# Products of zeros on TensorE in units 14 to 16 of a chunk of a scan-and-attention kernel

## The chip, the cores and the metric

The kernel runs on one core of one Trainium2 chip. The metric is the time on the device in microseconds (us). The engines are named as in the profile: PE is TensorE (PEld its weight loads), DVE is VectorE, ACT is ScalarE, POOL is GpSimd, and SP issues most of the DMAs.

## The reference

The input `x` has eight images of 96 channels and 64 x 64 places, so L = 4096 tokens each. What is computed, in short:

```python
# layer 0: group norm, then a selective scan (16 states, 192 inner channels)
xz = u @ in_proj_w.T                      # split in xm and z
xm = silu(causal_conv4(xm) + conv_b)
dt, Bm, Cm = split(xm @ x_proj_w.T)       # 6, 16 and 16 columns
delta = softplus(dt @ dt_proj_w.T + dt_proj_b)
h[t] = exp(delta[t] * A) * h[t-1] + delta[t] * Bm[t] * xm[t]   # 192 x 16 states
y[t] = sum_n h[t] * Cm[t] + xm[t] * D
x = x + layer_norm((y * silu(z)) @ out_proj_w.T)
# layer 1, on tokens
t = t + linear_attention(layer_norm(t))   # 6 heads, no softmax, so q (k^T v)
t = t + ffn(layer_norm(t))                # 96 -> 384 -> 96, fp8 e5m2 products, fp16 sums
```

## The kernel before, in words

Two images make a pair, and a pair is cut in eight **chunks** of T = 512 tokens: 4 pairs x 8 chunks = 32 chunks. A chunk is worked in 24 **units**. Unit `u` stands for a group `j` of 64 inner channels (3), a group `g` of four states (4), and an image `b` of the pair (2), in this order: `j = u // 8`, `g = (u // 2) % 4`, `b = u % 2`. A unit has two halves `h`, each of 128 rows (4 states x 32 channels) x 512 tokens.

What one unit does (function `unit`, in this order on its engines):

- PE copies the rows of C of the next unit into a PSUM bank (`rows_c`, L715, two banks `cc`), unless the unit is in `POOLED`.
- `steps(u, 0)`: the steps that the table `STEPS` lists before the bar for this unit.
- POOL multiplies delta * x by B three units ahead (`products_b`, L703, `dbu`).
- DVE scans both halves (L800, `hs`). After each half ACT writes the decay of the next unit's half, `exp(delta * A)`, into one of two PSUM banks `da` (`decay`, L725).
- In units 1, 9 and 17: `gate` (L766). DVE multiplies the finished sums of the group before by `silu(z)`.
- `steps(u, 1)`: the steps after the bar. In units 1, 9 and 17 then `skip` (L759): PE opens the bank `y` with `D * x` of the group `j` that begins.
- DVE multiplies the states by C (L823, `pr`), or POOL does so at the beginning of the next unit (`pooled`, L830), where the unit is in `POOLED`.

The **sums** over states are products on PE (`sums`, L747): for two units, four products with a 128 x 32 selection matrix, each added to 32 rows of the bank `y`, which stays open from `skip` until the fourth group of states has been added. A step `S` in the table runs the oldest of them, if its products are there. The bank `y` is single, its last sums are those of units 6 and 7, 14 and 15, 22 and 23, and `s["summed"]` is set to `j` when they have been issued. For j = 1 this happens in the two `S` steps of unit 16, part 0.

The steps of `STEPS` other than `S` advance generators of other work by one stage. The ones near the change:

- `P` (`chain_p`) prepares the chunk after the next: convolution (L491), z (L499), silu, then in units 13 to 17 the product with `x_proj` (L532), its copies on ACT (L537, L540), and three times a product of 12 rows for delta (L550) that ACT reads (L554) before the next can take the one bank `mp`. A softplus with its table loads (L555) follows on ACT.
- `E` (`chain_e`) takes the chunk before through output projection, layer norms and transposes. Its products with the input's tokens (L867) fall in units 13 and 14.
- `F0` and `F1` (`chain_f`) run the attention's output and the FFN of an earlier chunk, from the tenth chunk on. In `F0` the three products of the hidden layer (L1049) come first, then in unit 15 the second product (L1089, three fp8 products into bank `mF`), in unit 16 ACT's copy of it (L1094, `y16`), four transposes on PE (L1101) and the last addition on DVE (L1104).

Each engine works strictly in the order in which the program issues to it; the order is written out by hand in `STEPS` and `unit` (a manual schedule), with semaphores between the engines.

The parts of the table for the units of the change:

```python
    14: "F0 | E E P",
    15: "F0 F0 | P F0",
    16: "S S | P E F0 W1* F1 F0*",
```

Of the kernel before, what the change touches and what calls it, by code (L numbers as in the profile page):

```python
# [10 lines left out]
F16 = mybir.dt.float16  # L11
# [9 lines left out]
T = 512  # L21
# [38 lines left out]
    22: "F1 P F1 |",  # L60
    23: "E | P",
}


PAIRS = sorted({((u // 2) % NG, u % 2) for u in POOLED})
# [7 lines left out]
def tile_mamba_linear_attention_ffn(  # L73
# [29 lines left out]
    nc = tc.nc  # L103
    B, _, L = x.shape
# [4 lines left out]
    const = ctx.enter_context(tc.tile_pool(name="const", bufs=1))  # L109
# [299 lines left out]
    def now(kind):  # L409
        for work in waiting[kind]:  # L410
            work()
        waiting[kind].clear()
# [51 lines left out]
    here = {}  # L464
# [200 lines left out]
    def spread(s, j):  # L665

        if ("inputs", j) in s:
            settle(s["inputs", j])
        for to, of in (("du", "lu"), ("dl", "ld")):
            t = s[to, j] = p2.tile([128, 4, T], F32, tag=to, name=to)  # L670
            for n in range(NG):
                nc.sync.dma_start(
                    t[32 * n : 32 * n + 32],
                    s[of, j].rearrange("(q e) t -> e q t", e=32),
                )

    def rows_b(s, g):

        t = s["b", g] = p2.tile([128, 2, T], F32, tag="b", name="b", bufs=NG)
        for n in range(NG):  # L680
            nc.sync.dma_start(
                t[32 * n : 32 * n + 32],
                s["bd"][0 : 2 * NS].rearrange("(b n) t -> n b t", b=2)[NG * g + n]
                .unsqueeze(0)
                .to_broadcast([32, 2, T]),
            )

    def rows_pooled(s, g, b):

        t = s["c", g, b] = p2.tile([128, T], F32, tag=f"c{g}{b}", name="c", bufs=1)  # L690
        for n in range(NG):
            row = 2 * NS + NS * b + NG * g + n
            nc.sync.dma_start(
                t[32 * n : 32 * n + 32], s["bd"][row : row + 1].to_broadcast([32, T])
            )
# [4 lines left out]
    def products_b(s, u):  # L700
        j, g, b = where(u)
        dbu = s["dbu", u] = p2.tile([128, 2, T], F32, tag="dbu", name="dbu", bufs=AHEAD + 1)
        nc.gpsimd.tensor_mul(  # L703
            dbu, s["du", j][:, 2 * b : 2 * b + 2, :],
            s["b", g][:, b, :].unsqueeze(1).to_broadcast([128, 2, T]),
        )

    def rows_c(s, u):
        j, g, b = where(u)
        if u in POOLED:  # L710
            return
        if ("low", 0) in s:
            settle(s["low", 0])
        cc = s["cc", u] = ps_all.tile([128, T], F32, tag="cc", name="cc", bufs=2)
        nc.tensor.matmul(  # L715
            cc, lhsT=sel[64:128, g, b], rhs=s["cs"][64:128, :], start=True, stop=True
        )

    def decay(s, u, h, bank=None):
        if s is None or ("da", u, h) in s:  # L720
            return
        j, g, b = where(u)
        da = psum(bank) if bank else ps_all.tile([128, T], F32, tag="da", name="da", bufs=2)
        s["da", u, h] = da
        nc.scalar.activation(  # L725
            da, s["dl", j][:, 2 * b + h, :], AF.Exp, scale=aneg[:, 2 * j + h, g : g + 1]
        )
# [26 lines left out]
    def skip(s, j):  # L754

        s["open"] = j

        s["y"] = ps_all.tile([128, T], F32, tag="y", name="y", bufs=1)
        nc.tensor.matmul(  # L759
            s["y"], lhsT=dd[:, j, :], rhs=s["xm"][:, j, :], start=True, stop=False  # L760
        )

    def gate(s, j):
        assert s["summed"] == j
        zs = s["zs"][:, j, :]
        vector().tensor_mul(zs, s["y"], zs)  # L766

    def unit(s, prev, nxt, first, u, steps):
        def at(v):
            return (s, v) if v < NU else (nxt, v - NU)  # L770


        here.update(at=at, u=u, part=0)
        if u - 1 in POOLED:
            pooled(s, u - 1)
        elif not u and NU - 1 in POOLED and prev is not None:
            pooled(prev, NU - 1)
        if u:
            nc.scalar.copy(state["new"][:, u - 1, :], s.pop(("hs", u - 1))[:, :, T - 1])  # L779
        else:  # L780
            if prev is not None:
                nc.scalar.copy(state["new"][:, NU - 1, :], prev.pop(("hs", NU - 1))[:, :, T - 1])
            state["last"] = state.get("new")
            state["new"] = p2.tile([128, NU, 2], F32, tag="state", name="state")
        to, v = at(u + 1)
        if to is not None:
            rows_c(to, v)
        now("norms")
        steps(u, 0)
        to, v = at(u + AHEAD)  # L790
        if to is not None:
            products_b(to, v)
        now("shifts")
        if u % 2:
            due.append((s, u))
        hs = s["hs", u] = p2.tile([128, 2, T], F32, tag="hs", name="hs", bufs=3)
        dbu = s.pop(("dbu", u))
        to, v = at(u + 1)
        for h in range(2):
            nc.vector.tensor_tensor_scan(  # L800
                hs[:, h, :], s.pop(("da", u, h)), dbu[:, h, :],
                0.0 if first else state["last"][:, u, h : h + 1], ALU.mult, ALU.add,
            )
            if to is not None:
                decay(to, v, h)
        between[0] = 0
        now("others")

        new = u % (2 * NG) == 1
        if new and u > 1:  # L810
            gate(s, u // (2 * NG) - 1)
        elif new and prev is not None:
            gate(prev, NJ - 1)
        here["part"] = 1
        steps(u, 1)
        if new:
            skip(s, u // (2 * NG))
        if u in POOLED:
            return
        pr = s["pr", u] = p2.tile([128, 2, T], F32, tag="pr", name="pr", bufs=PRB)  # L820
        cc = s.pop(("cc", u)).unsqueeze(1)
        for lo, hi in ((0, 2),) if between[0] else ((0, 1), (1, 2)):
            nc.vector.tensor_mul(  # L823
                pr[:, lo:hi], hs[:, lo:hi], cc.to_broadcast([128, hi - lo, T])
            )

    def pooled(s, u):
        j, g, b = where(u)
        pr = s["pr", u] = p2.tile([128, 2, T], F32, tag="pr", name="pr", bufs=PRB)
        nc.gpsimd.tensor_mul(  # L830
            pr, s["hs", u], s["c", g, b].unsqueeze(1).to_broadcast([128, 2, T])
        )
# [338 lines left out]
    with tc.manual_schedule():  # L1171
        for u in range(AHEAD):
            products_b(slots[0], u)
        for h in range(2):
            decay(slots[0], 0, h)
        rows_c(slots[0], 0)
        for i, (p, c) in enumerate(chunks):
            s = slots[i]
            prev = slots[i - 1] if i else None
            nxt = slots[i + 1] if i + 1 < N else None  # L1180

            def steps(u, part):
                if part == 0:
                    if u in (0, 2 * NG):
                        spread(s, 1 + u // (2 * NG))
                    if nxt is not None and u == 18:
                        spread(nxt, 0)
                    if nxt is not None and u in ROWS_B:
                        rows_b(nxt, ROWS_B.index(u))
                    for k, v in ROWS_POOLED.items():  # L1190
                        if v % NU == u:
                            to = s if v >= NU else nxt
                            if to is not None and ("c", *k) not in to:
                                rows_pooled(to, *k)
                for name in (STEPS[u] + "|").split("|")[part].split():
                    step(name, i)

            for u in range(NU):
                unit(s, prev, nxt, c == 0, u, steps)
# [4 lines left out]
    s = slots[N - 1]  # L1204
# [285 lines left out]
```

## Time and profile before

| | |
|---|---|
| time, median of 3 runs | 3046.27 us (3036.72 to 3049.2) |
| profiled execution | 3054.44 us |
| its span, first to last instruction | 3052.7 us |
| mean granted TensorE clock | 0.807 |
| instructions in the span | 36480 |
| busiest engines | DVE 2822.1 us, POOL 2784.1 us |

A chunk takes some 90 us of the span, a unit some 3.7 us on the mean. The share of busy time is an average over the whole; what an engine's work is worth in one stretch is read from the waits there. Matmuls are pipelined and their ends are modelled, so that a busy PE row does not say that the array is full. The granted clock is the share of full speed that the core's throttle grants to TensorE, as the profile records it. In rows of the timeline the columns are the start, the duration, the engine, line and operation, what is written and read, the shape, the count of instructions merged, and in brackets the idle time before them with what ended it.

### The profile page before, as it was taken

To read this page: it belongs to the slowest core of one execution; us is meant where nothing else is said; L and a number is where in the kernel's file an instruction comes from. 1 tells how busy PE (TensorE), PEld (TensorE's weight loads), DVE (VectorE), ACT (ScalarE), POOL (GpSimd) and SP (SyncE) were. 2 spreads that over 40 slices of the span, in tenths; PEclk is the share of its full clock that TensorE was granted. 3 is DMA by queue.
4 is the path that set the end of the run, shared out by engine and by line. 5 is a ranking of instruction groups with operands and counts; after the bars stand their busy time and mean duration, and the time that the engine had idled before them with its cause. 6 is when DMAs were issued, how large, how long until landed. Compare 5 with 4: busy or idle time off the path is not lost. (4 is left out here: it accounts for less than half of the span.)

```text
span 3052.7 us, 36480 instructions
## 1 busy us (share of the span) xinstructions
PE 2413.1 (79%) x9663; PEld 931.8 (31%) x9663; DVE 2822.1 (92%) x4499; ACT 2384.0 (78%) x4809; POOL 2784.1 (91%) x1483
## 2 busy tenths in 40 slices
PE   5777777777788887787888778888887888888787
PEld 2122222222233332232333223232233333233355
DVE  4999999999999999999999999999999999999987
ACT  3666666777668888888888887888888888888766
POOL 2999999999999999999999999999999999999947
PEclk9787777777778888879887887888788888878679
DMA  5655666555576755657765556765556675555632
GB/s 138 144 139 139 160 164 160 143 130 128 134 170 173 179 150 147 148 127 170 182 168 142 140 150 152 178 171 143 135 139 145 171 180 144 139 133 129 165 99 78
DMA packets 261238, 452.24 MB, mean 148 GB/s; under 512 B 41701, under 2 KB 50086, under 8 KB 261030
## 3 DMA queue, kind: packets, MB, share of 16 engines
q1 hardware_dynamic: 256038, 447.81, 58.8%
q10 hardware_dynamic: 4992, 2.11, 0.3%
q8 instruction: 76, 1.25, 0.2%
q14 instruction: 132, 1.08, 0.1%
HBM read 357.50 MB, written 92.27 MB: 147 GB/s over the span
## 5 line engine op out<-in xcount | busy, mean ns | idle before, releaser
L703 POOL TENSOR_TENSOR dbu<-du,b 128x1024 f32<-128x1024 f32 x768 | 1828.5, 2410 | 52.0 <-DMA du<-lu 35.9
L800 DVE TENSOR_TENSOR_SCAN hs<-da,state,dbu 128x512 f32<-128x512 f32 x1290 | 1569.7, 1264 | 93.7 <-ACT da L725 92.8
L725 ACT ACTIVATE da<-dl,aneg 128x512 f32<-128x512 f32 x1474 | 989.8, 685 | 480.1 <-DVE hs L800 477.0
L830 POOL TENSOR_TENSOR pr<-hs,c 128x1024 f32<-128x1024 f32 x288 | 686.2, 2383 | 69.7 <-DVE hs L800 43.5
L823 DVE TENSOR_TENSOR pr<-hs,cc 128x512 f32<-128x512 f32 (+1 forms) x766 | 593.5, 805 | 0.0
L747 PE MATMUL y<-pr,ssum 128*32 128x512 f32 x3072 | 541.5, 799 | 4.9 <-POOL pr L830 4.9
L491 PE MATMUL mp<-u,wk 96*64 96x512 f32 x1488 | 420.6, 661 | 69.7 <-ACT xm L509 41.6
L715 PE MATMUL cc<-cs,sel 64*128 64x512 f32 x480 | 270.8, 579 | 3.9 <-DVE pr L823 3.4
L532 PE MATMUL mp<-xm,xpT 128*96 128x512 f32 x186 | 153.6, 993 | 120.1 <-ACT xm L525 77.0
L800 DVE TENSOR_TENSOR_SCAN hs<-da,dbu 128x512 f32<-128x512 f32 x184 | 212.6, 1203 | 25.3 <-ACT da L725 16.0
L550 PE MATMUL mp<-dbl,dtT 12*128 12x512 f32 x186 | 159.0, 948 | 72.4 <-ACT delta L554 36.4
L851 PE MATMUL mE<-woT,zs 128*128 128x192 f32 x744 | 151.0, 357 | 72.3 <-ACT t1e L859 46.9
L491 PEld LDWEIGHTS mp<-u,wk 96*64 96x64 f32 x1488 | 107.9, 146 | 290.2 <-issue 155.0
L759 PE MATMUL y<-xm,dd 128*128 128x512 f32 x192 | 130.1, 765 | 73.5 <-DVE zs L766 73.5
L715 PEld LDWEIGHTS cc<-cs,sel 64*128 64x128 f32 x480 | 100.1, 216 | 275.5 <-issue 168.8
L499 PE MATMUL mp<-u,wz 96*64 96x512 f32 x372 | 115.6, 704 | 63.2 <-ACT zs L522 58.6
L851 PEld LDWEIGHTS mE<-woT,zs 128*128 128x128 f32 x744 | 131.7, 206 | 95.7 <-ACT t1e L859 60.5
L747 PEld LDWEIGHTS y<-pr,ssum 128*32 128x32 f32 x3072 | 88.8, 128 | 211.2 <-issue 183.2
L779 ACT COPY state<-hs 128x2 f32<-128x2 f32 x736 | 133.7, 182 | 1.4
L532 PEld LDWEIGHTS mp<-xm,xpT 128*96 128x96 f32 x186 | 46.4, 270 | 234.1 <-ACT xm L525 129.6
L566 POOL TENSOR_TENSOR du<-delta,xm 128x512 f32<-128x512 f32 x93 | 117.5, 1280 | 0.0
L919 PE MATMUL mE<-t1e 128*97 128x97 f32 x496 | 74.1, 285 | 46.6 <-DVE gram L928 36.4
(326 smaller groups left out, 3272.0 us busy)
## 6 DMA issues: line engine op xcount, KB each, us to landing
du<-lu SPq DMA_DIRECT2D x380, 256.0 KB, 5.0
dl<-ld SPq DMA_DIRECT2D x380, 256.0 KB, 7.4
b<-bd SPq DMA_DIRECT2D x512, 128.0 KB, 3.5
lu<-du SPq DMA_DIRECT2D x96, 256.0 KB, 4.0
c<-bd SPq DMA_DIRECT2D x384, 64.0 KB, 3.5
ld<-delta SPq DMA_DIRECT2D x93, 256.0 KB, 3.0
xg<-in_x_dram SPq DMA_DIRECT2D x32, 384.0 KB, 3.6
xr<-in_x_dram SPq DMA_DIRECT2D x32, 384.0 KB, 8.4
```

The lines of the kernel that those rows point to most:

```text
L491: nc.tensor.matmul(ps[64 * b : 64 * b + 64, :], lhsT=wk[:, k, 64 * j : 64 * j + 64], rhs=u[:, b, k : k + T], start=(k == 0), stop=(k == 3),)
L532: nc.tensor.matmul(ps[0:C, :], lhsT=xpT[:, j, :], rhs=xm[:, j, :], start=(j == 0), stop=(j == NJ - 1),)
L550: nc.tensor.matmul(ps, lhsT=dtT[:, j, :], rhs=dbl[0 : 2 * RANK, :], start=True, stop=True)
L703: nc.gpsimd.tensor_mul(dbu, s["du", j][:, 2 * b : 2 * b + 2, :], s["b", g][:, b, :].unsqueeze(1).to_broadcast([128, 2, T]),)
L715: nc.tensor.matmul(cc, lhsT=sel[64:128, g, b], rhs=s["cs"][64:128, :], start=True, stop=True)
L725: nc.scalar.activation(da, s["dl", j][:, 2 * b + h, :], AF.Exp, scale=aneg[:, 2 * j + h, g : g + 1])
L747: nc.tensor.matmul(s["y"][q : q + 32, :], lhsT=ssum, rhs=pr[:, h, :], start=False, stop=(g == NG - 1),)
L779: nc.scalar.copy(state["new"][:, u - 1, :], s.pop(("hs", u - 1))[:, :, T - 1])
L800: nc.vector.tensor_tensor_scan(hs[:, h, :], s.pop(("da", u, h)), dbu[:, h, :], 0.0 if first else state["last"][:, u, h : h + 1], ALU.mult, ...
L823: nc.vector.tensor_mul(pr[:, lo:hi], hs[:, lo:hi], cc.to_broadcast([128, hi - lo, T]))
L830: nc.gpsimd.tensor_mul(pr, s["hs", u], s["c", g, b].unsqueeze(1).to_broadcast([128, 2, T]))
L851: nc.tensor.matmul(ps[:, 2 * k * C : 2 * (k + 1) * C], lhsT=zs[:, j, tok : tok + 128], rhs=woT[:, j].rearrange("p b c -> p (b c)"), start= ...
```

## The change

Two constants are filled with zeros in the set-up: `zw`, a weight of 128 x 128, and `zx`, an operand of 128 x 512, both in fp16. `zeros(n)` issues `n` products of them onto the open bank `y`, adding nothing to its values. It is called at the start of part 0 (after `rows_c` of the next unit, ahead of the steps) and of part 1 (ahead of the steps) of units 14, 15 and 16, with the counts 1 and 1, 2 and 2, 1 and 1. It returns without a product where no bank is open or the open group's sums have all been issued.

```diff
+ZEROS = {14: (1, 1), 15: (2, 2), 16: (1, 1)}
...
     def skip(s, j):
 
         s["open"] = j
-
+        here["sums"] = s
         s["y"] = ps_all.tile([128, T], F32, tag="y", name="y", bufs=1)
         nc.tensor.matmul(
             s["y"], lhsT=dd[:, j, :], rhs=s["xm"][:, j, :], start=True, stop=False
         )
+
+    zw = const.tile([128, 128], F16, name="zw")
+    nc.vector.memset(zw, 0.0)
+    zx = const.tile([128, T], F16, name="zx")
+    nc.vector.memset(zx, 0.0)
+
+    def zeros(n):
+        s = here.get("sums")
+        if s is None or s.get("summed") == s.get("open"):
+            return
+        for _ in range(n):
+            nc.tensor.matmul(s["y"], lhsT=zw, rhs=zx, start=False, stop=False)
...
         now("norms")
+        zeros(ZEROS.get(u, (0, 0))[0])
         steps(u, 0)
...
         here["part"] = 1
+        zeros(ZEROS.get(u, (0, 0))[1])
         steps(u, 1)
```

## The prediction

> **What bounds the kernel now.** I read the page first, then the chain of waits, then the stretch of units 13 to 19 of some chunks in order of time, and last the granted clock in that stretch. The page's first part and its clock row:
>
> ```profile
> PE 2413.1 (79%) x9663; PEld 931.8 (31%) x9663; DVE 2822.1 (92%) x4499; ACT 2384.0 (78%) x4809; POOL 2784.1 (91%) x1483
> PEclk9787777777778888879887887888788888878679
> ```
>
> VectorE (DVE) is busy for 2822 of 3053 us. TensorE (PE) has room on average, at a mean clock of 0.807. So a change on PE can move the end only where DVE waits. Who waits for whom, in total:
>
> ```profile
> ACT da L725 <- DVE hs L800: 477.0, 707, 4.6
> DVE hs L800 <- ACT da L725: 108.8, 120, 3.0
> DVE zs L766 <- PE y L747: 37.5, 28, 3.6
> ACT y L1094 <- PE mF L1089: 19.0, 39, 2.8
> ```
>
> DVE's scans wait 109 us for ScalarE's decays, its gate 37.5 us for the sums on PE, and ScalarE (ACT) waits 19 us for the FFN's second product. Where these waits stand in a chunk, from the timeline between 2178 and 2196 us:
>
> ```profile
> 2178.38 2.07 PE L550 MATMUL mp<-dbl,dtT 12*128 12x512 f32 x2 [1.09 <-ACT delta L554]
> 2180.39 1.52 PE L1089 MATMUL mF<-h,w2T 128*96 128x512 fp8e5 x3
> 2181.83 2.07 PE L550 MATMUL mp<-dbl,dtT 12*128 12x512 f32 x2
> 2181.94 0.58 ACT L1094 CAST y<-mF 96x512 f16<-96x512 f32 x1 [0.44 <-PE mF L1089]
> 2185.57 3.64 PE L747 MATMUL y<-pr,ssum 128*32 128x512 f32 x16
> 2189.33 0.69 DVE L766 TENSOR_TENSOR zs<-y,zs 128x512 f32<-128x512 f32 x1 [0.97 <-PE y L747]
> 2195.66 2.46 DVE L800 TENSOR_TENSOR_SCAN hs<-da,state,dbu 128x512 f32<-128x512 f32 x2 [0.65 <-ACT da L725]
> ```
>
> The bracket is the idle time before the group. From the first row to the sums (16 records, 3.64 us) PE does one thing after the other. ACT's cast of the FFN result (L1094) waits 0.44 us for PE. From that cast to the scan of unit 19 pass 13.7 us in 20 of the 21 chunks that have this cast and the next chunk's products, and in those 20 ACT has no other gap over 0.06 us on the way. DVE waits 0.97 us at the gate (unit 17) and 0.65 at the scan of unit 19: 1.62 us. In the chunk between 2449 and 2468 us the split is another and the sum the same:
>
> ```profile
> 2454.37 0.58 ACT L1094 CAST y<-mF 96x512 f16<-96x512 f32 x1 [0.44 <-PE mF L1089]
> 2461.05 0.69 DVE L766 TENSOR_TENSOR zs<-y,zs 128x512 f32<-128x512 f32 x1 [0.26 <-PE y L747]
> 2468.10 1.28 DVE L800 TENSOR_TENSOR_SCAN hs<-da,state,dbu 128x512 f32<-128x512 f32 x1 [1.36 <-ACT da L725]
> ```
>
> 0.26 + 1.36 = 1.62. So ACT's unbroken row of work, which starts at L1094, sets when unit 19 is scanned; a gate that opens sooner only makes the scan wait longer. What counts is whether L1094 comes sooner or later.
>
> The clock, in four stretches of 3.41 us (the step in which it changes in this trace) of the chunk from 1904 us; columns are busy time and count of PE, PEld, DVE, ACT, POOL, then the clock and DMA:
>
> ```profile
> 1903.70:1907.11 3.41, 3.31 (x11) 2.53 (x11) 3.11 (x4) 3.38 (x7) 3.25 (x3) 0.50 0.17 56
> 1907.11:1910.53 3.42, 3.42 (x6) 0.93 (x5) 3.42 (x5) 2.95 (x6) 3.42 (x3) 0.50 0.33 99
> 1910.53:1913.94 3.41, 3.41 (x11) 1.13 (x13) 3.41 (x19) 3.36 (x7) 3.41 (x2) 0.50 0.01 2
> 1913.94:1917.35 3.41, 3.41 (x17) 0.47 (x9) 2.56 (x3) 3.38 (x3) 2.92 (x2) 0.50 0.20 58
> ```
>
> PE is busy throughout, and the clock is 0.50 throughout.
>
> **The change, part by part.** *What runs.* Seven products a chunk, not eight: in part 1 of unit 16 the two S steps have just summed group j = 1, so `summed` equals `open` and `zeros` returns. 32 x 7 = 224 products with a weight load each. On PE they stand: two ahead of the second set of token products (L867) in unit 14, two ahead of the FFN's second product (L1089) in unit 15, two ahead of the third delta product (L550), one ahead of the sums in unit 16. The other engines keep their order but for set-up, and no wait is added. Two fills on DVE in the set-up: by the fill of 32x128 at 165 ns and the one of 1024 columns at 912 ns I estimate 0.4 us in all, where DVE waits 17.2 us for its first product anyway: nothing.
>
> *One zero's price.* No f16 product of 512 columns stands in the trace. The nearest is L1089, one byte a value and one record a product: three take 1.52 us, one alone 0.61 to 0.66, so each further one costs (1.52 - 0.62) / 2 = 0.45 us at clock 0.50. The other end is an f32 product, two records 0.85 us apart (L550: 2.07 us for two, 1.22 alone): 1.7 us. The lower end is nothing, in idle time. I take 0.45, since a zero is one record in the program, as L1089 is; 0.22 at clock 1.00.
>
> *Unit 14's pair, 0.9 us.* Idle time ahead of the second L550 follows it: 1.09 us in the chunk shown, 0.87 or more in 16 of the 21 chunks, 0.65 and 0.71 in two, at most 0.1 in three. So it is free in 18 and costs 0.9 us in three. In the first ten chunks (no FFN yet) it delays the second L550 by some 0.45, and ACT reads that 0.4 us or more after its end: free.
>
> *Unit 15's first pair, 0.9 us.* L1089 starts straight behind the second L550, whose last column sets it; the hidden values have been ready for 0.65 us or more in all 21. So it comes 0.9 us later, and ACT, which already waits there, passes 0.9 us to L1094 and everything behind it. This is the main term. Its cover would be a clock of 1.00.
>
> *Unit 15's second pair, another 0.9.* The third L550 is 1.8 us later. ACT reads it 0.6 us after its end and is itself 0.9 later: 1.8 - 0.9 - 0.6 = 0.3 more, if the clock stays at 0.50.
>
> *Unit 16's one and the sums.* At 0.50 the sums start 1.8 + 0.45 = 2.25 us later; at 1.00 they end sooner than now. The gate's wait grows from 0.97 to at most 3.2 us or vanishes; the chain on ACT leaves it 1.62 + 0.9 to 1.2 = 2.5 to 2.8. In the first case up to 0.7 us more can show. The ten chunks without the FFN have 0.4 us of room at the gate and some 2.4 us of waits at the scans behind it: nothing.
>
> *Whether the clock rises.* I added up for each 3.41 us stretch the columns that PE streamed times the share of the array's rows and columns in use (512 columns a record, twice that for f32). Above some 2,900 full columns the next stretch runs at 1.00, below at 0.50; that sorts 827 of 876 stretches rightly. L550 with its 12 rows counts 2 x 1024 x 12/128 = 192 in its 2.07 us, which is why PE is busy and slow. A zero counts 512. Around 2180 us a stretch runs from 2180.2 to 2183.6 and would take both pairs of unit 15 and L1089: 4 x 512 + 3 x 512 x 96/128 = 3,200, so the third L550 and the sums run at 1.00. Around 2454 us the border falls inside the first pair: some 2,800, and the clock stays. Either way L1089 has been delayed before it rises.
>
> The Trainium skill, "TensorE: Matmul & The Clock Gate", Part 1, says that PE goes from half to full clock after about 3.4 us of sustained busy time and back after an idle window of that length. The four rows above are busy and stay at 0.50, so by busy time the rule fails here; by that rule, filling the gaps would give full clock and the gain of the first rival.
>
> *The sum.* 18 chunks x 1.05 (between 0.9 and 0.9 + 0.3) + 3 x 2.1 (0.9 of unit 14 on top of 1.2) = 18.9 + 6.3 = 25 us. The profiled execution took 3054.4 us (span 3052.7), 8 us over the median of 3046.3; +25 us is 0.8%, so 3071 us on the median. Its own range: 12 us (clock up ahead of L1089 in half the chunks) to 45 (2.1 in all 21).
>
> **The rivals.** *The zeros hold the clock at 1.00 (not slower).* If the stretches of units 14 and 15 reach 2,900 columns with unit 14's pair, the second L550 takes 1.1 us in place of 2.07, L1089 0.7 less, the pairs 0.44 each, and ACT's 0.44 us vanish: 21 x 0.44 = 9 us off, 3037 us; no more, as the 1.62 us move and do not go. For it: units 12 to 14 are at 1.00 in many chunks. Against: the 12-row products count too little, and two zeros add 1,024 to stretches of some 1,600.
>
> *The zeros are hidden.* If L1089 waits for something other than the second L550, the pair fits ahead of it: 3046 us. Against: it starts at the last column of that product in each chunk read.
>
> *The sums become the bound.* If the clock stays at 0.50 to the end of the sums and a zero costs 0.7 us, the five that find no idle time put the sums 3.5 us later. The gate then waits 0.97 + 3.5 = 4.5 us, 2.9 over the 1.62 of now, in 21 chunks, and in the ten others 3.5 - 0.4 - 2.4 = 0.7: 61 + 7 = 68 us, 3114. It decides from about 0.5 us a zero. Against: the clock rises in part of the chunks.
>
> **How the numbers follow.** Forecast 0.60, clock held 0.14, hidden 0.14, sums 0.12. A difference of 0.5%, 15 us, is about what a measurement of this kernel can tell from none (the three runs spread by 0.4%). Slower by more: nearly nine tenths of the forecast and all of the sums' case, 0.65. Faster by more would need more than the 9 us: 0.07. Within: 0.28. The range from 3042 to 3096 leaves out most of the clock's case and the sums' case.
>
> **What would show it.** Right: ACT's wait at L1094 about 1.3 us in these chunks, unit 15 still at 0.50, the scan of unit 19 waiting longer, DVE's busy time unchanged, 7 records a chunk at 0.45 us. Wrong: a wait at L1094 at or under 0.44, or a clock near 1.00 in unit 15, or the gate's wait grown past the scan's.

## The result, and the profile after

The kernel after takes 3097.22 us, the median of four runs (3081.26 to 3107.14); the kernel before, run beside it, 3047.73 us (four runs, 3036.72 to 3050.18). The ratio is 1.0151, with a 95% interval of 1.0116 to 1.0185. So the change costs some 50 us by the medians and 46 by the ratio (which is estimated over the runs and is not simply the quotient of the medians), about twice the 25 us of the prediction. The median lies 1 us above its range of 3042 to 3096; the ratio on the 3046.27 us that the prediction started from gives 3092.

The profiled execution of after took 3107.14 us, the longest of its four runs; its span is 3105.4 us, 52.7 more than before's. In its lines everything stands a little lower in the file: the FFN's second product is L1106 (before: L1089), ACT's cast of it L1111 (L1094), the last addition L1121 (L1104), the delta product L553 and ACT's reading of it L557 (L550, L554), the sums L750 (L747), the gate L781 (L766), the scan L816 (L800), the decay L728 (L725). The zeros are L776. Chunks are counted from 0; those with the FFN's cast and the next chunk's products are 10 to 30, the "21 chunks" of the prediction.

The page's first part and its clock row:

```profile
PE 2495.0 (80%) x9887; PEld 968.1 (31%) x9887; DVE 2826.3 (91%) x4501; ACT 2388.4 (77%) x4809; POOL 2784.9 (90%) x1483
PEclk9687778787787888878788787778888877778789
```

224 more products on PE (9887 against 9663) and 82 us more of its time. DVE's busy time has grown by 4 us of the 52.7, so DVE waits. Its waits and ACT's, summed over the span (engine, waiting line, what ended the wait: us, times, longest):

```profile
DVE hs L816 <- ACT da L728: 103.2, 102, 2.8
DVE zs L781 <- PE y L750: 70.1, 34, 4.7
DVE res L1121 <- ACT delta L557: 22.3, 14, 2.2
ACT y L1111 <- PE mF L1106: 47.6, 42, 3.9
ACT delta L557 <- PE mp L553: 14.5, 27, 1.4
```

The gate's wait for the sums went from 37.5 to 70.1 us, ACT's wait at the cast from 19.0 to 47.6. Two waits are new: DVE's last addition (L1121, 22.3 us) and ACT's reading of the delta product (14.5 us). The third line names ACT's L557 because that event came last by the profile; the timeline shows what the addition waits for, four transposes (L1118) that stand on PE behind the third delta product. By the table `STEPS` they and ACT's cast are issued in unit 15, part 1, behind the step `P`; only the addition falls in unit 16. Chunk 20:

```profile
1928.80 2.07 PE L553 MATMUL mp<-dbl,dtT 12*128 12x512 f32 x2
1930.80 1.03 PE L776 MATMUL y<-zx,zw 128*128 128x512 f16 x2
1931.62 1.49 PE L1106 MATMUL mF<-h,w2T 128*96 128x512 fp8e5 x3
1932.90 1.06 PE L776 MATMUL y<-zx,zw 128*128 128x512 f16 x2
1933.15 0.58 ACT L1111 CAST y<-mF 96x512 f16<-96x512 f32 x1 [1.56 <-PE mF L1106]
1933.90 2.07 PE L553 MATMUL mp<-dbl,dtT 12*128 12x512 f32 x2
1935.90 1.09 PE L1118 MATMUL mF<-ident,x 128*96 128x128 f32 x4
1937.08 0.69 DVE L1121 TENSOR_TENSOR res<-mF,y 96x512 f32<-96x512 f32 x1 [1.72 <-ACT delta L557]
1937.64 0.61 PE L776 MATMUL y<-zx,zw 128*128 128x512 f16 x1
1938.18 3.64 PE L750 MATMUL y<-pr,ssum 128*32 128x512 f32 x16
1941.94 0.69 DVE L781 TENSOR_TENSOR zs<-y,zs 128x512 f32<-128x512 f32 x1 [1.81 <-PE y L750]
```

PE works without a gap from the first row to the sums. A pair of zeros takes 1.03 us and a lone one 0.61, so a further one costs 0.42. ACT's cast waits 1.56 us (0.44 in the chunks shown of before). Then DVE stands 1.72 us at the addition and 1.81 us at the gate, and no time at the scan of unit 19: 3.53 us in place of 1.62. The sums still run at half clock (16 in 3.64 us). Chunk 22 goes another way:

```profile
2123.57 1.03 PE L776 MATMUL y<-zx,zw 128*128 128x512 f16 x2
2124.40 1.49 PE L1106 MATMUL mF<-h,w2T 128*96 128x512 fp8e5 x3
2125.92 0.58 ACT L1111 CAST y<-mF 96x512 f16<-96x512 f32 x1 [1.24 <-PE mF L1106]
2126.67 1.23 PE L553 MATMUL mp<-dbl,dtT 12*128 12x512 f32 x2
2129.15 1.92 PE L750 MATMUL y<-pr,ssum 128*32 128x512 f32 x16
2131.54 0.66 DVE L781 TENSOR_TENSOR zs<-y,zs 128x512 f32<-128x512 f32 x1
2139.65 2.46 DVE L816 TENSOR_TENSOR_SCAN hs<-da,state,dbu 128x512 f32<-128x512 f32 x2 [2.38 <-ACT da L728]
```

Here the third delta product takes 1.23 us and the sums 1.92: the clock has risen, behind the FFN's product. The gate waits for nothing, and the whole of what is lost shows at the scan of unit 19: 2.38 us. The stretches of 3.41 us before and after that border (PE, PEld, DVE, ACT and POOL busy with counts, then the clock), first the three of chunk 20 from its second delta product on, then the one of chunk 22 that has both pairs of unit 15 in it:

```profile
1928.96:1932.38 3.42, 3.42 (x6) 1.07 (x7) 3.42 (x5) 2.53 (x5) 3.42 (x3) 0.50 0.25 87
1932.38:1935.79 3.41, 3.41 (x6) 0.80 (x4) 2.98 (x18) 2.59 (x5) 3.41 (x2) 0.50 0.01 2
1935.79:1939.20 3.41, 3.41 (x15) 1.40 (x18) 2.12 (x3) 3.17 (x3) 2.80 (x2) 0.50 0.16 44
2123.55:2126.96 3.41, 3.41 (x9) 1.33 (x9) 3.41 (x6) 2.14 (x4) 3.41 (x2) 0.50 0.01 2
```

In full-array columns, counted as in the prediction, the first three hold 1,867, 1,699 and 2,744 and the clock stays at 0.50 after each; the fourth holds 3,229 and the next stretch runs at 1.00.

**Where the 52.7 us went.** DVE's idle time by place, summed from the trace, in us ("four waits": last addition of unit 16, gate of unit 17, scans of units 18 and 19):

| place | before | after | growth | prediction |
|---|---|---|---|---|
| four waits, 21 chunks | 32.7 | 59.8 | 27.1 | 25 |
| four waits, chunks 0 to 9 | 25.5 | 31.6 | 6.1 | 0 |
| gate of unit 1, all chunks | 20.3 | 31.4 | 11.1 | not named |
| scans of units 5 and 23 | 5.2 | 12.1 | 6.9 | not named |
| DVE's busy time | 2822.1 | 2826.3 | 4.2 | 0 |

Together 55.4; the rest, in the start and the tail of the span and in small waits, is -2.7. Each column is one execution: before's is 8 us longer than the median on record with the prediction, after's 10 us longer than its own.

The third row belongs to work that the change does not touch. In chunk 20 of after the clock is at 1.00 in unit 0, and in chunk 21 at 0.50; the last sums of the group before (units 22 and 23) and the gate that needs them:

```profile
1873.00 1.92 PE L750 MATMUL y<-pr,ssum 128*32 128x512 f32 x16
1877.26 0.67 DVE L781 TENSOR_TENSOR zs<-y,zs 128x512 f32<-128x512 f32 x1
...
1968.99 3.64 PE L750 MATMUL y<-pr,ssum 128*32 128x512 f32 x16
1972.75 0.69 DVE L781 TENSOR_TENSOR zs<-y,zs 128x512 f32<-128x512 f32 x1 [3.36 <-PE y L750]
```

The gate waits 3.36 us or not at all. In before this happens in six chunks, five of them among the first ten (16.9 us there, 3.4 in the 21); in after in nine, seven of them among the 21 (7.6 and 23.7 us).

### The profile page after: what moved, and what is told of

Same layout as the page of the kernel before. It is cut to its first block, busy times and chain, and to the rows that moved or that the text cites. A ratio compares the mean times of both kernels' runs of the same rounds, so it can differ in the third digit from the quotient of the medians.

```text
span 3105.4 us, 36931 instructions
## 1 busy us (share of the span) xinstructions
PE 2495.0 (80%) x9887; PEld 968.1 (31%) x9887; DVE 2826.3 (91%) x4501; ACT 2388.4 (77%) x4809; POOL 2784.9 (90%) x1483
## 4 chain that ended last, share of the span: by engine, by line
DVE 35%; PE 23%; ACT 23%; issue 10%; DMA 5%; POOL 3%; SPq 2%; POOLq 0%; DVEq 0%; ACTq 0%
DVE hs L816 24%; DVE pr L840 6%; ACT da L728 5%; PE mp L553 4%; PE y L750 3%; PE mp L494 2%; ACT t1e L445 2%; PE y L776 2%; DMA b<-bd 2%; ACT L465 2%; DVE st L424 2%; PE mE L868 2%; DMA du<-lu 2%; PE cc L718 2%; ACT xm L528 1%
## 5 line engine op out<-in xcount | busy, mean ns | idle before, releaser
L706 POOL TENSOR_TENSOR dbu<-du,b 128x1024 f32<-128x1024 f32 x768 | 1830.1, 2413 | 59.3 <-DMA du<-lu 36.5
L816 DVE TENSOR_TENSOR_SCAN hs<-da,state,dbu 128x512 f32<-128x512 f32 x1290 | 1569.8, 1265 | 94.0 <-ACT da L728 90.5
L728 ACT ACTIVATE da<-dl,aneg 128x512 f32<-128x512 f32 x1474 | 990.4, 685 | 467.2 <-DVE hs L816 462.9
L750 PE MATMUL y<-pr,ssum 128*32 128x512 f32 x3072 | 524.2, 775 | 6.9 <-POOL pr L847 5.3
L494 PE MATMUL mp<-u,wk 96*64 96x512 f32 x1488 | 442.6, 701 | 64.0 <-ACT xm L512 39.2
L816 DVE TENSOR_TENSOR_SCAN hs<-da,dbu 128x512 f32<-128x512 f32 x184 | 212.6, 1205 | 21.8 <-ACT da L728 12.7
L553 PE MATMUL mp<-dbl,dtT 12*128 12x512 f32 x186 | 154.0, 919 | 48.6 <-ACT cs L543 40.9
L762 PE MATMUL y<-xm,dd 128*128 128x512 f32 x192 | 123.1, 727 | 72.5 <-DVE zs L781 72.4
L750 PEld LDWEIGHTS y<-pr,ssum 128*32 128x32 f32 x3072 | 86.1, 125 | 202.6 <-issue 179.3
L781 DVE TENSOR_TENSOR zs<-y,zs 128x512 f32<-128x512 f32 x96 | 64.7, 674 | 70.1 <-PE y L750 70.1
```

The source lines that it names most:

```text
L494: nc.tensor.matmul(ps[64 * b : 64 * b + 64, :], lhsT=wk[:, k, 64 * j : 64 * j + 64], rhs=u[:, b, k : k + T], start=(k == 0), stop=(k == 3),)
L553: nc.tensor.matmul(ps, lhsT=dtT[:, j, :], rhs=dbl[0 : 2 * RANK, :], start=True, stop=True)
L706: nc.gpsimd.tensor_mul(dbu, s["du", j][:, 2 * b : 2 * b + 2, :], s["b", g][:, b, :].unsqueeze(1).to_broadcast([128, 2, T]),)
L728: nc.scalar.activation(da, s["dl", j][:, 2 * b + h, :], AF.Exp, scale=aneg[:, 2 * j + h, g : g + 1])
L750: nc.tensor.matmul(s["y"][q : q + 32, :], lhsT=ssum, rhs=pr[:, h, :], start=False, stop=(g == NG - 1),)
L816: nc.vector.tensor_tensor_scan(hs[:, h, :], s.pop(("da", u, h)), dbu[:, h, :], 0.0 if first else state["last"][:, u, h : h + 1], ALU.mult, ...
```

## The experiments

Besides after, nine kernels were run, in three sets, each set beside its own runs of the kernel before. The last columns are from each kernel's profiled execution, in us: ACT's wait at the cast in the 21 chunks, the four waits in the 21 chunks, the same in chunks 0 to 9, and the gate of unit 1.

| kernel | median (runs) | before beside it | ratio, 95% interval | cast | four, 21 | four, 0-9 | gate 1 |
|---|---|---|---|---|---|---|---|
| before | | | | 9.0 | 32.7 | 25.5 | 20.3 |
| after | 3097.22 (4) | 3047.73 | 1.0151, 1.0116 to 1.0185 | 28.4 | 59.8 | 31.6 | 31.4 |
| e1 first pair | 3059.29 (7) | 3044.06 | 1.0050, 1.0033 to 1.0067 | 25.2 | 46.7 | 24.3 | 5.7 |
| e2 the others | 3064.38 (5) | 3044.06 | 1.0070, 1.0040 to 1.0101 | 10.4 | 43.8 | 24.4 | 17.1 |
| e3 thin | 3091.46 (4) | 3044.06 | 1.0154, 1.0118 to 1.0190 | 28.8 | 67.6 | 29.4 | 12.9 |
| e4 late | 3050.84 (10) | 3044.06 | 1.0019, 0.9995 to 1.0043 | 9.2 | 32.6 | 24.1 | 1.9 |
| e5 unit 14 | 3059.31 (10) | 3048.97 | 1.0034, 1.0013 to 1.0054 | 8.7 | 36.8 | 28.1 | 11.3 |
| e6 early chunks | 3044.76 (10) | 3048.97 | 0.9994, 0.9973 to 1.0015 | 9.5 | 33.6 | 24.4 | 9.3 |
| e7 four first | 3091.11 (4) | 3048.97 | 1.0129, 1.0102 to 1.0155 | 41.8 | 63.1 | 25.5 | 13.9 |
| e8 late apart | 3048.80 (12) | 3046.48 | 1.0006, 0.9992 to 1.0019 | 9.8 | 33.5 | 24.3 | 6.8 |
| e9 all and late | 3081.59 (5) | 3046.48 | 1.0126, 1.0105 to 1.0147 | 26.0 | 59.3 | 28.4 | 4.2 |

**e1, only the pair ahead of the FFN's second product.**

```diff
-ZEROS = {14: (1, 1), 15: (2, 2), 16: (1, 1)}
+ZEROS = {15: (2, 0)}
```

> Only the two zeros ahead of the FFN's second product (unit 15, part 0) are left: 64 products. Theory 1 (what stands ahead of that product delays ACT's cast of its result, and ACT's unbroken row behind the cast sets the scan of unit 19): ACT's wait at the cast grows from 9 us to about 28 us over the 21 chunks that have it, as with all zeros, and the four waits of DVE in units 16 to 19 together grow by 21 x 0.9 = 19 us; ratio to before 1.006, give or take 0.004 for the gate of unit 1. Rival (the sums are the bound): the sums come only 0.9 us later or are sped up, so less than 5 us. Rival (the zeros upset the clock's phase and nothing else): the four waits stay at 33 us.

It costs 15 us by the medians. In the profile ACT's waits at the cast come to 34.6 us over the span (19.0 before):

```profile
ACT y L1111 <- PE mF L1106: 34.6, 40, 2.3
```

Of that, 16.2 us more than before stand in the 21 chunks, 0.77 a chunk, and the four waits there grow by 14.0. A pair there delays ACT, and nearly all of the delay reaches DVE.

**e2, all but that pair.**

```diff
-ZEROS = {14: (1, 1), 15: (2, 2), 16: (1, 1)}
+ZEROS = {14: (1, 1), 15: (0, 2), 16: (1, 1)}
```

> The zeros of the change without the first pair of unit 15: 160 products. Theory 1: the cast's wait stays at 9 to 12 us, the four waits in units 16 to 19 grow by 3 x 0.9 for unit 14's pair and 21 x 0.3 for the pair ahead of the third delta product, 6 to 9 us in all; ratio 1.002 to 1.003. Rival (the sums are the bound): five sevenths of the zeros still delay the sums, so five sevenths of the loss, 30 us or more. Rival (phase of the clock): a loss as with all zeros, in the gate of unit 1.

The ratio is 1.007: more than the theory gave these zeros. The cast hardly waits longer (10.4 us in the 21 chunks against 9.0). What has grown is what stands behind the third delta product:

```profile
DVE res L1121 <- ACT delta L557: 11.5, 19, 1.4
DVE zs L781 <- PE y L750: 52.2, 37, 3.6
ACT delta L557 <- PE mp L553: 6.2, 25, 0.5
```

So the second pair and unit 16's zero reach DVE by a path of their own: PE, the transposes, the addition, and PE, the sums, the gate. In the 21 chunks the scan of unit 19 waits only 3.4 us (18.3 before), and in 12 of them not at all: there the sums have taken ACT's place as what comes last. e1 and e2 add 14.0 and 11.1 us to the four waits of the 21 chunks, after 27.1: on the whole the two parts add up.

**e3, the same zeros on 12 rows.**

```diff
-            nc.tensor.matmul(s["y"], lhsT=zw, rhs=zx, start=False, stop=False)
+            nc.tensor.matmul(s["y"], lhsT=zw[0:12], rhs=zx[0:12], start=False, stop=False)
```

> The same 224 products, but of 12 rows each (the weight and the operand cut to 12 partitions): the same time on PE and a tenth of the array. If the clock goes by the share of the array in use, thin zeros never raise it: units 16 and 17 stay at 0.50 in all chunks, the sums end late in all 21, and the four waits grow by 21 x (1.3 to 1.9) = 27 to 40 us, over the 27 us of the full zeros; ACT's wait at the cast stays at 28 us. If the clock goes by busy time alone, thin zeros raise it as often as full ones and nothing differs.

A thin zero is not shorter. The zeros' line of after and of e3 (ns min/median/max, then first and last start in us):

```profile
L776 PE MATMUL y<-zx,zw x224: 379/609/634, 121.7 to 2957.7; 128*128 128x512 f16 x112
```

```profile
L776 PE MATMUL y<-zx,zw x224: 374/626/629, 122.7 to 2952.0; 12*128 12x512 f16 x112
```

PE is busy for as long over the whole span too (after's line stands above):

```profile
PE 2502.6 (81%) x9887; PEld 964.3 (31%) x9887; DVE 2824.3 (91%) x4501; ACT 2390.1 (77%) x4809; POOL 2784.5 (90%) x1483
```

So a clock that went by busy time would act the same. It does not: in after the clock has risen by the time the sums begin in 7 of the 21 chunks, as in chunk 22; in e3 in none. (While the sums run it rises in four more chunks of after, in eight of e3 and in 13 of before.) The waits of e3 show what that does:

```profile
DVE res L1121 <- ACT delta L557: 31.3, 21, 2.7
DVE zs L781 <- PE y L750: 64.4, 37, 3.7
ACT y L1111 <- PE mF L1106: 42.3, 42, 3.3
```

The addition now waits in all 21 chunks (14 in after), and in none of them does the scan of unit 19. The four waits are 67.6 / 21 = 3.22 us a chunk. In after they are 3.26 in the 14 chunks whose clock was still low when the sums began and 2.03 in the seven others. So the rise of the clock gives back 7 x 1.2 = 8 us, too late and in too few chunks to pay for the zeros. The time itself does not tell e3 from after (1.0154 and 1.0151).

**e7, four zeros ahead of the FFN's second product and none elsewhere.**

```diff
-ZEROS = {14: (1, 1), 15: (2, 2), 16: (1, 1)}
+ZEROS = {15: (4, 0)}
```

> Four zeros in place of two ahead of the FFN's second product (unit 15, part 0), none elsewhere: 128 products. Theory 1 (their time goes into ACT's cast one to one, 0.45 us each while the clock is at 0.50): the cast's wait grows by 21 x 1.8 = 38 us over before's 9 (with two it grew by 16), less what a raised clock gives back on the last of them; the four waits of units 16 to 19 grow by about as much, 30 to 38 us; ratio 1.010 to 1.012. Rival (the pair only fills idle time and the loss is in the clock's phase): the same as with two, 1.005.

```profile
ACT y L1111 <- PE mF L1106: 67.3, 42, 3.9
```

In the 21 chunks the cast waits 41.8 us, 32.8 more than before, 1.56 a chunk; with two zeros it was 0.77. The price of a zero in this place, 0.39 us, is the same for the second two as for the first. The four waits grow by 30.4, so what ACT loses at the cast DVE loses behind it. This is the main term doubled and alone.

**e5, all four zeros in unit 14, ahead of the delta products.**

```diff
-ZEROS = {14: (1, 1), 15: (2, 2), 16: (1, 1)}
+ZEROS = {14: (2, 2)}
```

> Four zeros in unit 14 alone (two at the start of each part, all ahead of the second set of token products): 128 products, in a place where PE sits idle 0.9 to 1.3 us in 16 of the 21 chunks before it may begin the second delta product. Theory (clock by full columns, ACT's cast decides): 1,500 to 1,800 columns a stretch there plus 2,048 are over the threshold of 2,900, so the next stretch runs at 1.00, the second delta product takes 1.1 us in place of 2.1 and the cast's wait falls from 9 us towards 0: up to 9 us faster, ratio 0.997 to 1.000. Rival (zeros only cost time): 0.9 us at clock 1.00 fits the idle time in most chunks, ratio 1.000; where the clock is at 0.50 they cost 0.9 us more, 1.001 to 1.004.

This is the first rival with twice the zeros in its place. The mechanism exists: in 8 of the 21 chunks the clock rises before or in unit 15 and ACT's cast does not wait at all. In the others it waits up to 0.76 us in place of 0.44, because four zeros more than fill the idle time ahead of the second delta product, and the sum of it is 8.7 us against 9.0. The four waits grow by 4.1 us in the 21 chunks and by 2.6 in the first ten. The time is 0.3% above before. The gain that was hoped for did not come.

**e4, e6 and e8: zeros late in the chunk, for the gate of unit 1.** If the clock's state in units 22 to 1 sets that wait, zeros in units 21 to 23 should end it without touching units 14 to 16.

```diff
-ZEROS = {14: (1, 1), 15: (2, 2), 16: (1, 1)}
+ZEROS = {21: (1, 0), 22: (1, 0), 23: (1, 0)}
```

> One full zero at the start of each of units 21, 22 and 23, none in 14 to 16: 96 products. In before, six chunks wait 3.3 to 3.6 us each at the gate of unit 1 (20 us), and in those the clock is at 0.50 from unit 22 to unit 1 with 2,600 to 2,960 full columns a stretch, just under the threshold. If the threshold is on full columns, 512 more a stretch lift the clock there, the gate's wait in unit 1 falls from 20 us to under 5, and the kernel is faster by 10 to 20 us: ratio 0.994 to 0.997. If zeros only take PE's time, those chunks wait 3 x 0.45 us longer: 6 x 1.35 = 8 us slower.

```profile
DVE zs L781 <- PE y L750: 18.6, 20, 2.9
```

The gate of unit 1 waits 1.9 us in all (20.3 before). But the time is not lower: 1.0019, with 1 in the interval. In the profile the first ten chunks are 16.3 us shorter; in the 21 the scans of unit 23 wait 8.0 us longer and those chunks are 6.2 us longer in all. The zero of unit 22 stands on PE ahead of the FFN's first product (L1066), and ACT's cast of that product waits 31.4 us in unit 22 (22.1 in before), up to 5.4 in one chunk; the decays of unit 23 come behind it. e6 therefore keeps the three zeros to the first nine chunks (`LAG` is 9, and `here["chunk"]` is the chunk's number, set in the loop over chunks):

```diff
-        if s is None or s.get("summed") == s.get("open"):
+        if s is None or s.get("summed") == s.get("open") or here["chunk"] >= LAG:
```

> One zero at the start of each of units 21, 22 and 23, but only in the first nine chunks, where no FFN stage stands behind them on PE: 27 products. The run with such zeros in all chunks took the gate's wait of unit 1 from 16.9 to 1.9 us in the first ten chunks and made them 16 us shorter, and lost some of it in later chunks, where the zero of unit 22 stands ahead of the FFN's first product and the decays of unit 23 came late. Theory: the gain stays and the loss goes: 10 to 16 us faster than a run of before that has those waits, ratio 0.995 to 0.998. Rival (what the gate gains is paid back at once in the scans behind it): ratio 1.000.

The first ten chunks are again shorter, by 14.9 us, but the later ones 7.7 longer, most of it at the gate of unit 1 (6.7 us against 3.4): the wait has turned up in other chunks. The time is that of before. e8 has the three zeros in the first nine chunks and one, in unit 23, in the later ones:

```diff
-ZEROS = {14: (1, 1), 15: (2, 2), 16: (1, 1)}
+ZEROS = {23: (1, 0)}
+EARLY = {21: (1, 0), 22: (1, 0), 23: (1, 0)}
...
-        zeros(ZEROS.get(u, (0, 0))[0])
+        zeros((EARLY if here["chunk"] < LAG else ZEROS).get(u, (0, 0))[0])
...
```

(The call of part 1 is changed in the same way.)

> No zeros in 14 to 16. In the first nine chunks one zero at the start of units 21, 22 and 23, in the later ones one at the start of unit 23 alone, behind the FFN's first product: 50 products. Theory (the gate of unit 1 waits 3.4 us in those chunks whose stretch before the sums stays just under the threshold, and one zero lifts it): the gate's wait in unit 1 is under 5 us in all chunks, 15 us less than in the profiled run of before, and nothing else grows; ratio 0.995 to 0.998. Rival (a zero in unit 23 delays the next transposes and with them other work of ACT): the decays of unit 23 or 0 come later and eat it: 0.999 to 1.002.

The gate of unit 1 falls to 6.8 us, 13.5 less than in before's profile; the time stays (1.0006, 0.9992 to 1.0019), which is the rival's range. In the first ten chunks the gate waits 15.5 us less but DVE idles only 9.1 us less: 6.4 us came back in small waits, of which the scans of unit 23, with 2.3, are one. The profiled execution of before was 8 us above its median, so a part of its 20.3 us may be of that one execution. None of the three is a faster kernel.

**e9, the change and e8 together** (the calls as in e8).

```diff
-ZEROS = {14: (1, 1), 15: (2, 2), 16: (1, 1)}
+ZEROS = {14: (1, 1), 15: (2, 2), 16: (1, 1), 23: (1, 0)}
+EARLY = {14: (1, 1), 15: (2, 2), 16: (1, 1), 21: (1, 0), 22: (1, 0), 23: (1, 0)}
```

> All zeros of the change and those of the run before in addition. Theory: the change's loss is the sum of two, the four waits of units 16 to 19 (33 us more in its profile) and the gate of unit 1 (11 us more, by the phase at which the clock's stretches meet the chunk). The late zeros take the second away and not the first: the gate's wait in unit 1 under 5 us, the four waits at 85 to 95 us in all, ACT's wait at the cast at 28 us; ratio to before 1.008 to 1.011 in place of 1.015. Rival (the waits of units 16 to 19 also come from the phase): both change at random and the ratio stays at 1.013 to 1.018.

The ratio falls between what the two theories gave. With 50 more zeros the median is lower, 3081.6 us against after's 3097.2, but the two intervals of the ratio overlap, so a shorter time is not shown. Its five runs lie within 4.1 us (3081.0 to 3085.14), after's four within 26. In the profile the gate of unit 1 takes 4.2 us in place of 31.4, and the four waits of the 21 chunks hardly change (59.3 against 59.8):

```profile
DVE zs L782 <- PE y L751: 44.3, 28, 4.6
DVE res L1122 <- ACT delta L558: 19.8, 14, 2.1
```

The scans of unit 5 wait 10.6 us longer than in before. Between the two profiles the span is 25.5 us shorter and the gate of unit 1 waits 27.2 us less; but after's profile is of the longest of its four runs. By the medians some 14 of the 50 us go away with the late zeros, by the ratios some 8 of 46: how much of the loss in a usual run of after goes with that gate is not shown. e3 warns against putting it high: its time is after's, and in its profile that gate waits 12.9 us, less than in before's.

## Why the prediction was right, and where it was too small

**The direction, and the main term.** ACT's row of work from the cast sets the scan of unit 19, and a pair ahead of the FFN's second product delays the cast: predicted 0.9 us a chunk, measured alone 0.77 (e1), doubled 1.56 (e7), and DVE pays for it (14.0 and 30.4 us). With all zeros the cast's wait grows by (28.4 - 9.0) / 21 = 0.92, the other zeros adding the rest. The signs put forward for it are there: a wait of about 1.3 us at the cast (28.4 / 21 = 1.35), and the clock at 0.50 at the FFN's product in all 21 chunks. Chunk 22 shows the row of work as the prediction read it: the gate's wait is gone and the scan's is 2.38, against 1.62 + 0.9 = 2.5.

**Seven products a chunk at 0.45 us.** 224 records; a further one costs 0.42 us at half clock. DVE's busy time grew by 0.15%. These steps hold. The trace of before does have products in f16 of 512 columns, contrary to what the prediction says: nine in the tail (L1400), 0.38 us each at full clock and 0.59 for the one in which the clock falls. They would have given the price of a lone zero (0.61 at half clock), not that of a further one.

**The clock.** 2,900 full-array columns a stretch sort 835 of 891 stretches of after rightly, and 844 of 890 of e3; it is a fit, and near the border it errs. The rise came where the tally put it, behind the FFN's product, in a part of the chunks: 7 of 21. The Trainium skill, "TensorE: Matmul & The Clock Gate", Part 1, has the clock released by about 3.4 us of sustained busy time. In after PE is busy for 99% or more of a stretch at half clock 247 times, and 131 times the next stretch is at half clock again. e3 is the test without a model: the same busy time on 12 rows, and no rise ahead of the sums. The measurement decides: busy time alone does not set the clock here, the share of the array in use counts.

**The size of the four waits: near in sum, by errors that cancel.** The sum was made of 1.05 us in 18 chunks and 2.1 in three. Measured are 1.70 us in 14 chunks (3.26 less 1.56, before's mean) and 0.47 in seven: 23.8 + 3.3 = 27.1. That this is close to 25 is partly luck: 14 chunks cost more than the 1.05 and seven less. The prediction had the 14 in hand: at half clock "up to 0.7 us more can show", with the sums 2.25 us later. That gives 0.97 + 2.25 = 3.22 us, which is also the mean of e3's 21 chunks (2.3 to 4.0 each). But the 0.7 was put in no term of the sum. The prediction also lets the sums decide only "from about 0.5 us a zero"; its own lines set that lower, where 0.97 + 5z passes 1.62 + 2z + 0.3, at 0.32 us. In ten of the 14 chunks the scan of unit 19 does not wait: the second pair and unit 16's zero set the end, not ACT (e2 shows their path). In the other four the clock rises while the sums run, and the scan still waits 0.2 to 0.7 us. The sign of being wrong, "the gate's wait grown past the scan's", came true: gate and addition 43.4 us in the 21 chunks, scan 16.4. The sign of being right, a longer wait at that scan, is seen in the seven chunks whose clock rose (1.0 to 2.4 us each, 0 to 1.4 before); in sum it fell, from 18.3. The last addition itself, behind the transposes, was not named.

**The first ten chunks: 6.1 us, predicted nothing.** The room was there but smaller than the delay: the gate of unit 17 grew from 2.2 to 17.0 us, and the scans behind it gave back 8.7.

**What was put at nothing.** The prediction summed only waits in units 14 to 19 and took the rest of the chunk as it was. Outside its sum after's profile has the 6.1 us of the first ten chunks, 6.9 at the scans of units 5 and 23, 4.2 of busy time on DVE, and 11.1 at the gate of unit 1.

The last of these depends on the clock's stretches. When a chunk becomes longer, their borders fall elsewhere in the next one. Where the clock stays low from unit 22 on, the sums of units 22 and 23 run at 0.50 and the gate waits 3.4 us. That the clock sets this wait is shown by chunks 20 and 21 above and by e4, e8 and e9, where zeros in those units take it away (to 1.9, 6.8 and 4.2 us). The tally of columns is too coarse to say which chunk waits: in after stretches of 2,633 to 2,689 columns there (chunks 15, 20 and 25) were followed by full clock, and stretches of 3,022 (chunks 16 and 21) by half. The start of the chunk against the border says more. In before, after, e1, e2, e3, e5, e6 and e7 together, 27 of the 168 chunks from 10 to 30 have their first scan 1.36 to 1.61 us behind a border; 17 of them wait over 2.5 us at this gate, and of the 141 others none does. Of after's 21 chunks ten start there and seven wait, of before's two and one. So after's profile has more waits because more of its chunks start in that part of a stretch. A chunk that is a whole number of stretches long (3.413 us each) hands its start on to the next: in after chunks 27 and 28 are 95.53 and 95.49 us long (28 stretches are 95.57), and 27, 28 and 29 wait; in before chunks 2 to 4 are 88.75 us long (26 stretches are 88.75), and 2 to 5 wait.

That the change itself brings chunks there is not shown. In e3, with zeros of the same length in the same places, two of the 21 wait, in e7 one. So a part of the 11.1 us may be of the one execution that was profiled, and the 50 us of the medians are accounted for only to within some ten.

**The rivals.** "Hidden" falls: the cast waits longer in all 21 chunks. "The clock held" falls for this change; with four zeros in unit 14 it happens in 8 of 21 chunks (e5) and gains nothing over all. "The sums become the bound" is right as a mechanism in ten of 21 chunks and in part in four more, but wrong in its price, since a zero costs 0.42 and not 0.7 us: 1.7 us a chunk over the 14, not 2.9.

## What to carry to other kernels

Before filling idle time on an engine, look which wait ends last behind each place: where an engine works without a gap, a product put in delays what stands behind it by about its length, and on PE at half clock that was 0.4 us here even where it computes nothing. What raised the clock was work that fills the array, and the reward came one stretch later; if the critical product stands before that border, it pays and does not gain. And when one stretch of a repeated piece changes length, look again at the other stretches that stand close to the clock's border: they may flip, and a single profile shows one draw of them.

## What was not expected of the hardware

Products on 12 rows take PE as long as products on 128 (626 and 609 ns, medians) and leave the clock at 0.50. A wait of 3.4 us in one chunk and none in the next, with the same instructions, goes with the clock alone. Whether it makes up much of the scatter of the runs is open: after's four lie within 26 us and e9's five, with that wait nearly gone, within 4, but e4's ten, with 1.9 us of it in the profile, lie within 18. The 19 runs of before beside e5, e6 and e7 lie between 3038 and 3063 us.
